# A two-layer adjacency kernel: the rows' score constants and the final tests moved to the end, one ScalarE pass per adjacency block, and records scattered later

## The chip, the cores and the metric

The kernel runs on one core of a Trainium2 chip. The metric is device time in microseconds, the median of several executions. Lower is better. TensorE is called PE in the profile, VectorE DVE, ScalarE ACT, GpSimd POOL and SyncE SP.

## The reference

There are 2708 nodes with 1024 features, a sparse 0/1 adjacency matrix, and two layers:

```python
# layer 0
q = x @ W_q.T + b_q;  k = x @ W_k.T + b_k;  v = x @ W_v.T + b_v
z = (q @ k.T) / 32 * adj
z = where(z == 0, -10000, z)
x = layernorm(x + relu(softmax(z, axis=1) @ v))
# layer 1
x = layernorm(x + adj @ (x @ weight) + bias)
```

## The kernel before

The function `sparse_part` treats the adjacency as lists of neighbours; after it a branch on `flag` runs `dense_part` only if one of the tests made by the sparse part has failed. With these inputs the branch is not taken. The nodes are 22 blocks of 128 rows (the last has 20). The stages overlap and are written in this order:

1. **Weights.** W_q and W_k are turned on TensorE, and M = scale W_q^T W_k is formed by 28 half-size products (`product_of_m`, seven for each of four blocks, the scheme of Strassen and Winograd).
2. **Listing.** `list_columns` handles a block of adjacency rows: it is loaded in six column ranges, each followed by eight ones that serve as an end mark. ScalarE counts the nonzero elements with a Sign pass, and looks for negative ones with a Relu pass (`neg`). VectorE finds up to eight ones in each range (`max_index`), and sorts their places into `keys`. Three buffers `a` go round, and `a_tile` has GpSimd set the ones in each of them anew. Sixteen blocks (`EARLY`) are listed during M's products, the rest during y's first pairs.
3. **Sorting.** Rows are ordered by degree in two families (blocks 0 to 7 and the rest): `sort_begin`, `sort_end`, then `records_out` scatters each row's record of neighbours into `tab_ds` from GpSimd, and reads it back as `tabs` and `tab0`. `records_back` makes masks of them.
4. **y = x M + a row.** Four pairs of blocks go through `y_pair`, in seven half products each, of which the third to sixth use sums of x (`y_sums_of`, on GpSimd) and four also differences of M (`t1` to `t4`, on VectorE). The other blocks go through `y_block`. The row of biases adds `y_col`. The score of row i with neighbour j is y_i . x_j plus a constant of row i, c_i = x_i . u + b, where u comes from b_k and W_q. Before, c_i is formed beside the pairs: `load_rows_of_c` loads x again, `row_constants` multiplies it by `u_bc`, and c_i is stored behind y's row, which is therefore 1028 elements wide (`YW`).
5. **Layer 0.** For each sorted block, `attend` gathers the neighbours' rows of x by indirect DMA from GpSimd, forms scores, a softmax and the weighted sum on VectorE, and pairs of blocks are projected by W_v (`project_pair`). A constant of a row doesn't change its softmax; it is needed for the tests only. Rows with one neighbour (`single`, blocks 18 and 19) need no score for their result; their score is formed by a second job of `attend_one`, for the test alone.
6. **The tests** (L1348 to L1378): scores equal to zero, degrees over the slots, a maximum that is so low that masked entries would count. A matmul with ones collects them, and `values_load` gives the flag to each engine.
7. **Layer 1.** Ten units of two blocks: `sum_rows` gathers neighbours, `work1` multiplies by the weight, `finish1` normalizes and scatters the result.

Every engine takes its instructions in the order of its own queue. A scheduler fixes these orders beforehand, by program order and its own expectation of when an instruction's inputs are there; `tc.high_priority` draws evictions from PSUM (`add`) forward, and `follow(later, earlier)` makes an instruction wait for another. `products` holds the last matmul of each block or unit, `began` the first matmul of each half product. `p_tr` is a ring of three PSUM banks, `p_mm` one bank, `p_o` four banks for products. The names and lines that the prediction uses: L213 ones, L231 and L232 ScalarE's passes, L235 `max_index`, L241 part of the listing, L308 `add`, L379 to L382 `y_sums_of`, L659 in `sort_end`, L679 the scatter of records, L712 in `records_back`, L761 a sum for M, L767 a copy of M's products, L789 and L809 `t3` and `t4`, L921 scatter, L1445 layer 1's evictions.

Of the kernel before, what the change touches and what calls it, by code (L numbers as in the profile page):

```python
# [9 lines left out]
F32 = mybir.dt.float32  # L10
BF16 = mybir.dt.bfloat16
I32 = mybir.dt.int32
U16 = mybir.dt.uint16
# [7 lines left out]
P = 128  # L21
# [59 lines left out]
def sparse_part(ctx, tc, x, xT, adj, wqT, wkT, wvT, bq, bk, bv, w1, b1, out):  # L81
# [14 lines left out]
    YW = D + 4  # L96
# [5 lines left out]
    y_ds = [dram.tile([n, YW], F32, name=f"y{f}_d") for f, n in enumerate((FAMILY * P, N - FAMILY * P))]  # L102
# [8 lines left out]
    with es:  # L111
# [81 lines left out]
        neg = lists.tile([P, NB], F32, name="neg")  # L193
        keys = lists.tile([P, NB, KEYS], F32, name="keys")
        nc.vector.memset(cnt, float(8 * RANGES))
        nc.vector.memset(neg, 0.0)
# [12 lines left out]
        def a_tile():  # L209

            a = la.tile([P, AW], F32, name="a")
            for i in range(RANGES):
                nc.gpsimd.memset(a[:, cuts[i + 1] + 8 * i:cuts[i + 1] + 8 * i + 8], 1.0)  # L213
            return a

        def load_adj():
            b = len(loaded)
            if b < NB:
                a = a_tile()
                for i in range(RANGES):  # L220
                    load_rows(a[:, cuts[i] + 8 * i:cuts[i + 1] + 8 * i], adj[:, cuts[i]:cuts[i + 1]], b * P, rows[b])
                loaded.append(a)
# [3 lines left out]
        def list_columns():  # L226
# [4 lines left out]
            nc.scalar.activation(junk[:n], a[:n], AF.Sign, accum_out=cnt[:n, b:b + 1])  # L231
            nc.scalar.activation(junk[:n], a[:n], AF.Relu, scale=-1.0, accum_out=neg[:n, b:b + 1])  # L232
# [15 lines left out]
        b_bc = a_tile()  # L248
# [224 lines left out]
        top2 = const.tile([P, 2], F32, name="top2")  # L473
        bad = const.tile([P, 1], F32, name="bad")
# [148 lines left out]
        def sort_begin(f):  # L623
# [9 lines left out]
            nc.vector.tensor_scalar(capn, neg[:, bs], 0.0, 1.0e6, op0=ALU.is_gt, op1=ALU.mult)  # L633
            nc.vector.tensor_add(deg[:, bs], deg[:, bs], capn)
# [11 lines left out]
        def sort_end(f, behind=None):  # L646
            b0, nb = families[f]
            bs, NKB = slice(b0, b0 + nb), NK * nb
            before = spare_bank()
# [75 lines left out]
        def product_of_m(acc, a, w, start, stop):  # L725
# [8 lines left out]
            if not sorted_ and done > FAMILY + 2 and worked > 7 * DC // 2 - 4:  # L734
                records_out(*sort_end(0, put), 0, FAMILY)
                sorted_.append(0)
# [75 lines left out]
        c_all = stat.tile([P, NB, YW - D], F32, name="c_all", bufs=1)  # L812
        nc.vector.memset(c_all, 0.0)
        y_bc = xa.tile([P, YW], F32, name="y_bc", bufs=1)
        bcast_rows(y_bc, y_col)
        u_bc = xa.tile([P, D], F32, name="u_bc", bufs=1)
        mm = p_mm.tile([P, HALF], F32, name="mm")
        nc.tensor.matmul(mm[:, :1], ones, bqk, start=True, stop=True)
        nc.vector.memset(y_bc[:, D:], 0.0)
        nc.vector.tensor_copy(y_bc[:, D:D + 1], mm[:, :1])  # L820


        deal = deal_hub()
        junkc = lists.tile([P, D], U8, name="junkc")
        c_ready, c_blocks = [], list(range(NB))

        def load_rows_of_c():
            a = la.tile([P, AW], F32, name="a")
            for k in range(2):
                b = c_blocks.pop(0)  # L830
                load_rows(a[:, k * D:(k + 1) * D], x, b * P, rows[b])
                c_ready.append((b, a[:, k * D:(k + 1) * D]))

        def row_constants(count):
            for _ in range(count):
                b, xg = c_ready.pop(0)
                n = rows[b]
                nc.vector.scalar_tensor_tensor(junkc[:n], xg[:n], 1.0, u_bc[:n], op0=ALU.mult, op1=ALU.mult,
                                               accum_out=c_all[:n, b, 0:1])
                if b in (FAMILY - 1, NB - 1):  # L840
                    f = int(b >= FAMILY)
                    b0, end = families[f][0], sum(families[f])
                    nc.vector.tensor_scalar(c_all[:, b0:end, 0], c_all[:, b0:end, 0], y_bc[:, D:D + 1], None, op0=ALU.add)
                    full = min(end, NB - 1)
                    nc.sync.dma_start(out=y_ds[f][:(full - b0) * P, D:].rearrange("(b p) e -> p b e", p=P), in_=c_all[:, b0:full])
                    if full < end:
                        nc.sync.dma_start(out=y_ds[f][(full - b0) * P:, D:], in_=c_all[:rows[full], full])
# [8 lines left out]
        for b in range(0, FAMILY, 2):  # L856
            while done < min(NB, EARLY + 4 * (b // 2 + 1)):
                list_columns()
                done += 1
            y_pair(b)  # L860
            if b == 0:
                bcast_rows(u_bc, u_col)
# [5 lines left out]
            row_constants(len(c_ready))  # L868
            for _ in range({2: 4, 4: 5, 6: 2}.get(b, 0)):
                load_rows_of_c()  # L870
# [5 lines left out]
        for b in range(FAMILY, FAMILY + 2):  # L876
# [4 lines left out]
            row_constants(len(c_ready))  # L881
            load_wv(range(2 * (b - FAMILY), 2 * (b - FAMILY) + 2))
        assert not c_ready and not c_blocks
# [32 lines left out]
        def gather_y(b):  # L916
            yg = wp.tile([P, YW], F32, name="yg")
# [96 lines left out]
        def score(yg, xg, s, n):  # L1014
            nc.vector.scalar_tensor_tensor(junkv[:n], yg[:n, :D], scale, xg[:n], op0=ALU.mult, op1=ALU.mult,  # L1015
                                           accum_out=s)

        def masked_scores(b, j0, s, yg, less):
# [3 lines left out]
            nc.vector.scalar_tensor_tensor(z, s, yg[:n, D:D + 1], less, op0=ALU.add, op1=ALU.add)  # L1022
# [6 lines left out]
        def attend(b, got):  # L1029
# [4 lines left out]
            for i, (j0, j1) in enumerate(cut):  # L1034
# [5 lines left out]
                z = masked_scores(b, j0, s[:n, :m], yg, less[:n, b, j0:j1])  # L1040
# [53 lines left out]
        def attend_one(b, got):  # L1094
# [7 lines left out]
            yg = gather_y(b)  # L1102
            xg = gather(x, b, 0, n)
            s = stat.tile([P, 1], F32, name="s1")
            score(yg, xg, s[:n], n)
            masked_scores(b, 0, s[:n], yg, less[:n, b, 0:1])
            yield
# [14 lines left out]
        def attend_shares(b, got):  # L1122
# [7 lines left out]
            yg = wp.tile([P, YW], F32, name="yg")  # L1130
            gather_at(y_ds[0][:, :], rec[:, OFF:OFF + 1], P, yg)
            for i, (j0, j1) in enumerate(pieces(J)):
# [5 lines left out]
                z = masked_scores(b, j0, s[:, :m], yg, far_less[:, j0:j1])  # L1138
# [98 lines left out]
        late_jobs = [7, 19, 18, 8, 8, 17, 8, 16, 11, 15, 10, 9, 14, 19, 13, 12, 18]  # L1237
# [110 lines left out]
        cap = stat.tile([P, NB], F32, name="cap", bufs=1)  # L1348
        for b in range(NB):
            nc.vector.memset(cap[:, b:b + 1], float(SLOTS[b]))  # L1350
        nc.vector.memset(cap[:HUB, 0:1], 1e9)
        nc.vector.memset(cap[HUB:2 * HUB, 0:1], float(ROW))
        if rows[-1] < P:
            nc.vector.memset(cap[:, NB - 1:NB], 1e9)
            nc.vector.memset(cap[:rows[-1], NB - 1:NB], float(SLOTS[-1]))
        over = stat.tile([P, NB], F32, name="over", bufs=1)
        nc.vector.tensor_tensor(over, degs, cap, op=ALU.is_gt)
        s0, b0 = slot0[single[0]], single[0]
        nc.vector.scalar_tensor_tensor(nms[:, b0:b0 + len(single)], scores[:, s0:s0 + len(single)], -1.0,
                                       valid[:, b0:b0 + len(single), 0], op0=ALU.mult, op1=ALU.mult)  # L1360

        nc.vector.tensor_scalar(scores, scores, 0.0, None, op0=ALU.is_equal)
        zero = stat.tile([P, 1], F32, name="zero", bufs=1)
        nc.vector.tensor_reduce(zero, scores, AX.X, ALU.max)
        nc.vector.tensor_max(bad, bad, zero)
        low = stat.tile([P, NB], F32, name="low", bufs=1)
# [433 lines left out]
```

## Time and profile before

| | us |
|---|---|
| median of 3 runs (1079.43 to 1086.11) | 1081.06 |
| the profiled execution | 1078.39 |
| its span, first to last instruction | 1076.7 |
| TensorE busy in it | 967.3 (90%) |
| VectorE | 854.9 (79%) |
| GpSimd | 529.4 (49%) |
| ScalarE | 432.2 (40%) |

The profile is of one execution; its own time is that of the span and 1.7 us around it. Durations below are from it. In its lines, "out<-in" are the program's tile names without buffer numbers, "x8" is a count, and brackets hold the idle time of the engine before the instruction and what ended it. A row of waits reads: who waited, for whom, us in total, times, longest.

### The profile page before, as it was taken

Reading aid. Unit: us, or ns where it says so; the run is one execution under the profiler, and the core shown is the slowest. Engines: PE = TensorE matmul, PEld = TensorE weight load, DVE = VectorE, ACT = ScalarE, POOL = GpSimd, SP = SyncE. Lnnn points to the kernel's source line nnn. Section 1 sums busy time; section 2 is a strip of 40 time slices with the busy share of each in tenths; the row PEclk is TensorE's granted clock in tenths of the full one; section 3 lists DMA queues with packets and bytes.
Section 4 is the critical chain, followed back from the end, with each engine's and each line's share of the span. In section 5 each row is a group of like instructions: output and inputs, shape, how many; then the busy total and the mean of one; then the engine's idle time right before and its main releaser. Section 6 shows DMA issues by size and latency. Waiting matters only on the chain.

```text
span 1076.7 us, 10650 instructions
## 1 busy us (share of the span) xinstructions
PE 967.3 (90%) x2697; PEld 454.8 (42%) x2697; DVE 854.9 (79%) x2071; ACT 432.2 (40%) x902; POOL 529.4 (49%) x552
## 2 busy tenths in 40 slices
PE   7998859899999798768999999999499899989893
PEld 6443424344444343333554444444254344435441
DVE  8999969996485897999999998844469777867532
ACT  4598866525221322231633333322323243353521
POOL 0441073123167774555565766210388777768510
PEclk9998979999999899888999999999799999999997
DMA  9558875799846767645645777334597699987731
GB/s 353 163 172 246 246 206 150 242 310 315 297 148 199 254 206 235 188 135 162 221 129 196 246 235 255 120 112 134 196 272 238 202 299 285 329 244 211 216 93 42
DMA packets 105782, 228.80 MB, mean 213 GB/s; under 512 B 22500, under 2 KB 49900, under 8 KB 105710
## 3 DMA queue, kind: packets, MB, share of 16 engines
q0 software_dynamic: 48192, 147.52, 43.4%
q1 hardware_dynamic: 57518, 80.50, 23.5%
q8 instruction: 23, 0.38, 0.1%
q14 instruction: 49, 0.40, 0.1%
HBM read 217.60 MB, written 33.68 MB: 233 GB/s over the span
## 4 chain that ended last, share of the span: by engine, by line
DVE 21%; issue 15%; PE 14%; DMA 12%; POOL 9%; ACT 1%; POOLq 0%; DVEq 0%
PE po L291 13%; DVE junkv L1015 4%; DMA g<-x_d,tabs 4%; POOL g L459 4%; DVE r L1072 3%; DMA g<-in_x_dram,tabs 2%; DVE t L308 2%; DMA yg<-y_d,tabs 2%; POOL xr L451 1%; DVE t L1220 1%; DVE r L1156 1%; DMA g<-x_d,tab 1%; DVE r L1408 1%; DVE part L1408 1%; POOL yg L451 1%
## 5 line engine op out<-in xcount | busy, mean ns | idle before, releaser
L366 PE MATMUL po<-m,xt 128*128 128x512 f32 x416 | 185.3, 606 | 10.5 <-DVE yo L308 10.4
L291 PE MATMUL po<-t,s_all 128*128 128x512 f32 x320 | 150.2, 613 | 14.8 <-DVE xr L308 10.4
L1015 DVE SCALAR_TENSOR_TENSOR junkv<-yg,g 128x1024 uint8<-128x1024 f32 x108 | 131.9, 1221 | 38.6 <-DMA g<-in_x_dram,tabs 18.7
L459 POOL DMA_INDIRECT g<-in_x_dram,tabs x84 | 108.9, 1296 | 61.2 <-issue 12.8
L366 PEld LDWEIGHTS po<-m,xt 128*128 128x128 f32 x416 | 79.9, 194 | 113.2 <-issue 97.1
L1408 DVE SCALAR_TENSOR_TENSOR r<-g,valid,r 128x1024 f32<-128x1024 f32 x77 | 98.1, 1280 | 15.4 <-DMA g<-x_d,tabs 14.1
L291 PEld LDWEIGHTS po<-t,s_all 128*128 128x128 f32 x320 | 61.6, 195 | 98.7 <-issue 72.7
L459 POOL DMA_INDIRECT g<-x_d,tabs x66 | 76.8, 1164 | 23.2 <-issue 16.5
L977 ACT ACTIVATE junks<-t,lnm 128x1024 uint8<-128x1024 f32 (+1 forms) x40 | 45.9, 1148 | 104.5 <-DVE lnm L975 103.4
L935 ACT COPY rT<-tr 128x512 f32<-128x512 f32 x76 | 41.5, 588 | 109.3 <-PE tr L934 107.9
L235 DVE FIND_INDEX8 at_a<-ones,a 128x8 uint16<-128x83 f32 (+3 forms) x132 | 82.6, 628 | 0.0
L1072 DVE SCALAR_TENSOR_TENSOR r<-g,pr,r 128x1024 f32<-128x1024 f32 x64 | 81.6, 1279 | 0.6 <-ACT r L1070 0.3
L291 PE MATMUL po<-wv,s_all 128*128 128x512 f32 x160 | 75.4, 615 | 4.1 <-DVE s_all L1195 3.7
L440 ACT ACTIVATE junka<-xt 128x128 f32<-128x128 f32 x168 | 51.6, 307 | 64.9 <-PE po L291 33.4
L291 PE MATMUL po<-w,rT 128*128 128x512 f32 x160 | 73.7, 602 | 2.0 <-DVE t L1445 2.0
L291 PE MATMUL po<-t,rT 128*128 128x512 f32 x160 | 73.9, 604 | 0.0
L291 PE MATMUL po<-w,s_all 128*128 128x512 f32 x160 | 72.2, 592 | 0.0
L291 PE MATMUL po<-wv,rT 128*128 128x512 f32 x160 | 70.6, 592 | 0.0
L231 ACT ACTIVATE junk<-a 128x2756 uint8<-128x2756 f32 (+1 forms) x22 | 55.1, 2502 | 29.2 <-DMA a<-in_adj_dram 13.7
L990 ACT ACTIVATE t<-t,nmr,rstd 128x1024 f32<-128x1024 f32 (+1 forms) x40 | 48.7, 1237 | 35.4 <-DVE nmr L989 32.9
L213 POOL MEMSET a<- 128x8 f32 x138 | 6.2, 107 | 112.8 <-DVE junk L282 39.4
L921 POOL DMA_INDIRECT x_d<-t,tabs x22 | 27.4, 1246 | 60.6 <-ACT t L990 52.6
(395 smaller groups left out, 1751.3 us busy)
## 6 DMA issues: line engine op xcount, KB each, us to landing
xt<-in_xT_dram SPq DMA_DIRECT2D x21, 512.0 KB, 6.3
y_d<-yo SPq DMA_DIRECT2D x21, 512.0 KB, 5.0
a<-in_x_dram SPq DMA_DIRECT2D x21, 512.0 KB, 5.9
a<-in_adj_dram SPq DMA_DIRECT2D x21, 413.5 KB, 5.6
a<-in_adj_dram SPq DMA_DIRECT2D x21, 338.5 KB, 4.4
a<-in_adj_dram SPq DMA_DIRECT2D x21, 263.5 KB, 4.4
wq_i<-in_wqT_dram SPq DMA_DIRECT2D x8, 512.0 KB, 6.4
wk_i<-in_wkT_dram SPq DMA_DIRECT2D x8, 512.0 KB, 10.2
```

The costliest lines, as they stand in the source:

```text
L231: nc.scalar.activation(junk[:n], a[:n], AF.Sign, accum_out=cnt[:n, b:b + 1])
L235: nc.vector.max_index(at[:n, i], ones[:n, :8], a[:n, cuts[i] + 8 * i:cuts[i + 1] + 8 * i + 8])
L291: put = nc.tensor.matmul(acc, a[:, k], w[:, k], start=start and k == 0, stop=stop and k == DC // 2 - 1, skip_group_check=True)
L366: put = nc.tensor.matmul(po, xts[b][:, c, :], m_q[c // 4][h][:, c % 4], start=(c == 0), stop=(c == DC - 1))
L440: put = nc.scalar.activation(junka[:, :xt.shape[2]], xt[:, c, :], AF.Copy, accum_out=xs[:, c, b:b + 1])
L459: nc.gpsimd.indirect_dma_start(out=dst[:n], out_offset=None, in_=src, in_offset=bass.IndirectOffsetOnAxis(ap=at, axis=0), bounds_check=N - ...
L935: nc.scalar.copy(rT[:, g * 4:g * 4 + 4, :], tr)
L977: nc.scalar.activation(junks[:n], t[:n], AF.Square, bias=nm[:n], accum_out=vs[:n])
L990: applied.append(nc.scalar.activation(t[:n], t[:n], AF.Identity, bias=nmr[:n], scale=rstd[:n]))
L1015: nc.vector.scalar_tensor_tensor(junkv[:n], yg[:n, :D], scale, xg[:n], op0=ALU.mult, op1=ALU.mult, accum_out=s)
L1072: nc.vector.scalar_tensor_tensor(r[:n], xg[j][:n], pr[:n, j:j + 1], r[:n], op0=ALU.mult, op1=ALU.add)
L1408: put = nc.vector.scalar_tensor_tensor(r[:n], xg[:n], ok[:n, j:j + 1], r[:n], op0=ALU.mult, op1=ALU.add)
```

## The change

- **One ScalarE pass per block.** The Relu pass and `neg` are gone. The Sign pass reads the same bits as unsigned integers, so that a negative number counts as well as a positive one; whether this reading holds is tested once with -1 (`minus`, `seen`).
- **Ones set once.** The three buffers `a` are fixed tiles, and the ones behind the ranges are set when a buffer is first used.
- **First records later.** `sort_end(0)` stays in M's products, but `records_out` for the first family is called after `y_pair(0)`, behind the first matmul of that pair's second half product. In `sort_end(0)` the first sum takes `p_mm`'s bank instead of one of `p_tr`.
- **Rows' constants in layer 1.** The loads of x, the products with u, `c_all` and the wider rows of y are gone from stage 4; `masked_scores` adds the mask only. In the last two units of layer 1, x's rows are gathered by sorted row and multiplied by u (`c_rows`): twelve after the ninth unit's last matmul (`products[-1]`), eleven after the tenth's. `u_bc` is formed in the eighth unit.
- **Single blocks' scores** are formed in the last two units as well (`single_scores`), not in layer 0.
- **The tests** come after the last `finish1`, and add `c_rows` to the scores, slot by slot, before they compare them.

```diff
-            nc.scalar.activation(junk[:n], a[:n], AF.Sign, accum_out=cnt[:n, b:b + 1])
-            nc.scalar.activation(junk[:n], a[:n], AF.Relu, scale=-1.0, accum_out=neg[:n, b:b + 1])
+            nc.scalar.activation(junk[:n], a[:n].bitcast(U32), AF.Sign, accum_out=cnt[:n, b:b + 1])
...
-        def a_tile():
-            a = la.tile([P, AW], F32, name="a")
+        a_bufs = [la.tile([P, AW], F32, name=f"a{k}", bufs=1) for k in range(3)]
+        def ones_behind_ranges(a):
             for i in range(RANGES):
                 nc.gpsimd.memset(a[:, cuts[i + 1] + 8 * i:cuts[i + 1] + 8 * i + 8], 1.0)
...
-                a = a_tile()
+                a = a_bufs[b % 3]
+                if b < 3:
+                    ones_behind_ranges(a)
...
-            before = spare_bank()
+            before = spare_bank() if f else p_mm.tile([P, HALF], F32, name="mm")
...
-                records_out(*sort_end(0, put), 0, FAMILY)
-                sorted_.append(0)
+                sorted_.append(sort_end(0, put))
...
+            first = len(began)
             y_pair(b)
             if b == 0:
-                bcast_rows(u_bc, u_col)
+                records_out(*sorted_[0], 0, FAMILY, began[first + 1])
                 records_back(0)
...
-            row_constants(len(c_ready))
-            for _ in range({2: 4, 4: 5, 6: 2}.get(b, 0)):
-                load_rows_of_c()
...
-            nc.vector.scalar_tensor_tensor(z, s, yg[:n, D:D + 1], less, op0=ALU.add, op1=ALU.add)
+            nc.vector.tensor_add(z, s, less)
...
-        late_jobs = [7, 19, 18, 8, 8, 17, 8, 16, 11, 15, 10, 9, 14, 19, 13, 12, 18]
+        late_jobs = [7, 19, 18, 8, 8, 17, 8, 16, 11, 15, 10, 9, 14, 13, 12]
...
+        def row_constants(ks, behind):
+            for k in ks:
+                n = P if k in (0, NB) else rows[k]
+                at = rec_h[:, ROW:ROW + 1] if k == NB else tab0[:, ROW:ROW + 1] if k == 0 else tabs[:n, k, ROW:ROW + 1]
+                xg = gather_at(x, at, n, g_tile(), behind=behind)
+                nc.vector.scalar_tensor_tensor(junkv[:n], xg[:n], 1.0, u_bc[:n], op0=ALU.mult, op1=ALU.mult,
+                                               accum_out=c_rows[:n, k:k + 1])
+
+        def single_scores(b):
+            n = rows[b]
+            yg = gather_at(y_ds[b >= FAMILY][:, :], tabs[:n, b, OFF:OFF + 1], n, g_tile())
+            xg = gather(x, b, 0, n)
+            s = stat.tile([P, 1], F32, name="s1")
+            score(yg, xg, s[:n], n)
+            masked_scores(b, 0, s[:n], less[:n, b, 0:1])
...
             pending = list(zip(unit, *work1(unit, *turned1.pop(i), xrs.pop(i))))
+            if i == len(units) - 3:
+                u_bc = wp.tile([P, D], F32, name="r", bufs=RB)
+                bcast_rows(u_bc, u_col)
+            if i >= len(units) - 2:
+                row_constants(range(i % 2, NB + 1, 2), products[-1])
+                single_scores(single[i % 2])
...
         for p in pending:
             finish1(*p)
+        cap = stat.tile([P, NB], F32, name="cap", bufs=1)
...
+        mm = p_mm.tile([P, HALF], F32, name="mm")
+        nc.tensor.matmul(mm[:, :1], ones, bqk, start=True, stop=True)
+        nc.vector.tensor_scalar(c_rows, c_rows, mm[:, :1], None, op0=ALU.add)
+        for k, (b, slots) in enumerate(list(enumerate(SLOTS)) + [("hub", HUB_SLOTS)]):
+            if slots:
+                z = scores[:, slot0[b]:slot0[b] + slots]
+                nc.vector.tensor_scalar(z, z, c_rows[:, k:k + 1], 0.0, op0=ALU.add, op1=ALU.is_equal)
+        nc.vector.tensor_sub(nms, nms, c_rows[:, :NB])
...
+        nc.vector.tensor_scalar(flag, mm[:1, 0, :1], 0.0, None, op0=ALU.is_gt)
+        raised = nc.values_load(flag, min_val=0, max_val=1, skip_runtime_bounds_check_because="a comparison's result")
```

## The prediction, made before the changed kernel ran

> **What bounds the kernel now.** I read the totals first, then the busy time by stage (cut at the steps of TensorE's work), then the waits inside the stage the change touches, then the queues of GpSimd and VectorE there, last the end of the span.
>
> ```profile
> PE 967.3 (90%) x2697; PEld 454.8 (42%) x2697; DVE 854.9 (79%) x2071; ACT 432.2 (40%) x902; POOL 529.4 (49%) x552
> ```
>
> TensorE is the bound on average; ScalarE, whose passes are halved, is at 40%. By stage (columns: stretch, length, busy time of PE, PEld, DVE, ACT, POOL, clock, DMA share, GB/s):
>
> ```profile
> 27.00:131.35 104.35, 99.02 (x235) 44.18 (x234) 104.09 (x363) 81.95 (x73) 27.71 (x100) 0.97 0.67 204
> 131.35:157.00 25.65, 9.86 (x27) 4.77 (x24) 22.06 (x82) 20.92 (x28) 15.99 (x23) 0.81 0.85 248
> 176.30:204.80 28.50, 25.69 (x64) 10.98 (x63) 28.40 (x116) 24.80 (x66) 6.31 (x11) 1.00 0.70 212
> 513.00:764.00 251.00, 243.94 (x693) 116.53 (x691) 204.58 (x485) 94.71 (x178) 114.81 (x88) 0.99 0.56 183
> 1017.00:1060.30 43.30, 43.16 (x96) 18.75 (x96) 15.69 (x49) 11.97 (x18) 7.86 (x7) 0.96 0.28 75
> ```
>
> To see: while the weights' product M is formed (27 to 131) VectorE is as full as TensorE (104.09 of 104.35); its load is the listing of adjacency columns. From 131 to 157 TensorE works 9.86 of 25.65. The last unit's time (1017 on) is TensorE alone. What TensorE waited for between 131 and 256:
>
> ```profile
> PE po L291 <- POOL y_s L380: 10.9, 1, 10.9
> PE tr L187 <- DVE upto L659: 4.9, 1, 4.9
> PE po L291 <- DVE yo L308: 3.9, 6, 1.2
> ```
>
> The first is GpSimd's queue, the order in it being the cause:
>
> ```profile
> 139.12 1.14 POOL L679 DMA_INDIRECT tab_d<-rec,pos_i  x1 [2.93 <-DVE at_a L235]
> 148.23 2.79 POOL L679 DMA_INDIRECT tab_d<-rec,pos_i  x1 [0.30 <-issue]
> 151.26 3.28 POOL L379 TENSOR_TENSOR y_s<-xt 128x512 f32<-128x512 f32 x1
> ```
>
> Eight record scatters (139.1 to 151.0) stand ahead of the sums that y's first pair needs. What would be late next, on VectorE:
>
> ```profile
> 147.89 2.28 DVE L789 TENSOR_TENSOR y_t<-y_t,m 128x2048 f32<-128x2048 f32 x1
> 151.15 2.26 DVE L809 TENSOR_TENSOR y_t<-m,y_t 128x2048 f32<-128x2048 f32 x1
> 162.63 0.69 DVE L308 TENSOR_TENSOR yo<-po,y_bc 128x512 f32<-128x512 f32 x1 [9.21 <-PE po L291]
> ```
>
> The weights' differences t3 (L789) and t4 (L809) end at 150.2 and 153.4, only behind the sixteenth listed block. The end of the span:
>
> ```profile
> 1060.33 0.69 DVE L1445 SCALAR_TENSOR_TENSOR t<-po,xr 128x512 f32<-128x512 f32 x1 [1.43 <-PE po L291]
> 1064.75 0.95 POOL L921 DMA_INDIRECT out_dram<-t,tabs  x1 [5.17 <-ACT t L1008]
> L77 POOLq INC_SWDGE_SEM  x1: 1620/1620/1620, 1068.3 to 1068.3; - x1
> L1796 POOLq DRAIN  x3: 50/107/5867, 1069.9 to 1076.4; - x3
> ```
>
> The last matmul ends at 1060.3, and 16.4 us follow: the last block's norm and scatter (landed about 1068), 1.62 and 5.87 us of GpSimd's closing.
>
> **What the Trainium skill says.** "TensorE: Matmul & The Clock Gate", What's actually happening: after an idle window of about 3.4 us the array runs at half clock until it has been busy as long. The trace agrees: after the 10.9 us wait 24 matmuls took 12.35 us, against 24 x 0.429 = 10.3. "SBUF — State Buffer", SBUF: two separate sides: a GpSimd operation and a VectorE one with two SBUF inputs lock each other out. Agrees: L241 took 1.18 us beside GpSimd's L761 at 61.1, 0.20 at 136.5. "ScalarE: Activation LUTs", The pipeline for one element: 0.833 ns an element, whatever the function. A pass over 2756 would be 2.30 us and a fixed part; the rows show 2.50. It says nothing of uint32 input. "DMA: Bandwidth & Descriptors", Where 436 GB/s comes from: 435 GB/s at the ports, some 358 at HBM. The nine gathers at 254.9 to 266 ran with 408 GB/s moving (266 to 270), so the measurement stands above the lower figure.
>
> **The change part by part.** Sums are against the profiled execution (1078.39 us, span 1076.7); the median shown is 2.67 us above it.
>
> *One ScalarE pass.* 22 x (2.50 + 0.19) = 59 us of ScalarE go. In the M stage ScalarE's copy L767 came late behind listing passes: TensorE waited 5.3 us at 95, and ran cold after it. That alone could end M 4 to 7 us sooner. The uint32 Sign pass isn't in the trace: no faster than the 2.30 above, and taken at 2.50; at 5.0 the saving is gone, with nothing lost.
>
> *Ones set once.* 114 of 138 memsets of 0.1 us leave GpSimd, and each load then waits for VectorE and ScalarE only, and by ranges. Cost nothing; VectorE never starved for blocks there, so no gain by itself.
>
> *Records later; another bank for sort_end.* The scatters (8 x 1.28 + 1.5 = 11.9 us) go behind the second product of pair 0, so the sums come first. Their input xt was issued at 129.0; xt lands in 6.3 (its issue row), so 135.3; three operations at 1.28 give S1 at about 139.5. The transposes of y_bc no longer wait for L659 (4.9). TensorE then does products 1 and 2 by 137 to 139, product 3 from 140. Product 5 needs t3. VectorE was full from 27 on, and the change takes next to nothing from it before 147, so t3 stays: 147.89 + 2.28, and two evictions of 0.68 now fall ahead of it: 151.5. Products 5 to 7 are 3 x 8 x 0.429 = 10.3: pair 0 ends at 161.8, where it ended at 176.3. **Gain 14.5**, not the 24 of all waits. If the listing of one more block (its searches, 3.77, and small operations: about 5.5 us) is ordered ahead of t3, 9 remain; if t3 is drawn ahead, 19. The tables arrive later (they landed by 166, first read at 185.9, gathers begin at 254.9): covered, or about 5 us if VectorE reaches L712 first.
>
> *Row constants out of y's pairs.* 22 products of 1.30 leave VectorE between 202 and 257, 10.6 MB of loads leave SP's queue, and y's rows are 4096 bytes. Pairs 2, 4 and 6 took 28.5, 25.5 and 25.0 where 56 matmuls of 0.429 are 24.0: 6.1 lost, of it 0.9 the transposes of u_bc. Pair 2's is the listing, which stays; I take **3** of it, 0 to 6. The 0.9 comes back in layer 1. Later stages follow TensorE and only shift.
>
> *Two single blocks' scores out of layer 0.* 3 us of VectorE and four gathers; TensorE is at 244 of 251 there: **1**, between -1 and 3.
>
> *The old tests* were 1.6 us at 691 to 692.7 on an idle VectorE, and a matmul at 761 that nothing waited for: nothing.
>
> *Twelve constants after unit 8's last matmul.* GpSimd issues 12 gathers at 1.30 in the last unit's 24 us, where it was busy 7.9 of 43: they fit. The 12 products (15.6 us) fit VectorE too, but stand in its queue ahead of evictions while a gather is in flight (5.7 from issue to landing). TensorE has four banks, two products' slack: **+1.5**, 0 to 4.
>
> *Eleven constants after unit 9's last matmul.* This is bare, as no matmul is left. Zero is the last matmul's end. Eleven gathers at 1.30: the last is issued at 13.2, lands at 18.4 (I take 5.2, between 4.45 for the first gather of layer 1 and 5.7), its product ends at 19.8. Then c_rows' addition 0.2; 21 small operations at 0.10 spacing 2.1; subtractions and the old chain of tests 2.1; matmul and flag 0.7: 24.9. Before, the flag was known at 762; now GpSimd's load of it (0.50), its waits (0.8) and closing (1.62 + 5.87 + 0.8) follow: 34.5 instead of 16.4. **+18.1**, between +15 (part of the drain covered) and +22. The last block's scatter, behind eleven gathers on GpSimd, lands by 21 and is hidden.
>
> Sum: -14.5 - 3 - 1 + 1.5 + 18.1 = +1.1, so 1079.5 profiled, **1082 us** against the median.
>
> **Rivals.** *Slower: VectorE's listing takes the waits' place.* ScalarE no longer spaces the blocks, so two blocks (11 us) come ahead of t3, which ends at 162.5; pair 0 then gains 3.5, and the sum is +12: 1093. It decides from the second block on. For it: VectorE is full from 27 to 153. Against it: L789's inputs were ready by then and blocks 17 on stood behind it.
> *Faster: all waits go and the end is short.* 5.3 + 4.9 + 10.9, 4 of cold clock, 5 of the pairs less what t3 keeps is 26; the end at +15, two scores 2: -13, so 1068. For it: each wait has its own row. Against it: t3's time, and POOL's 1.30 a gather.
>
> **How the numbers follow.** Cancelling 0.46, the listing 0.33, all waits gone 0.21. A difference under 1% is about what a measurement of this kernel can't tell from none, so these are also within, slower, faster. The bounds of the likeliest give 1070 to 1094; with the rivals' outer parts, 1068 to 1097.
>
> **What would show it.** Right: pair 0's last product ends about 15 us sooner, with a wait on L789's line; no row POOL y_s L380 in TensorE's waits; some 34 us between the last matmul and the end, with eleven gathers in a row at 1.3 on GpSimd. Wrong: the end under 28 us, or pair 0 ending before 156 or after 168.

## The result, and the profile after

The changed kernel takes 1093.57 us (median of 5 runs, 1091.26 to 1097.20), the kernel before 1081.38 (5 runs, 1079.43 to 1086.11): a ratio of 1.0106, 95% interval 1.0073 to 1.0139. It is about 1.1% slower. The forecast was 1082.0, no change; the time lies in its range, 1068 to 1097, near the time of the slower rival. The profiled execution of the changed kernel took 1091.26 us with a span of 1089.4, against 1078.39 and 1076.7. The ratios and their intervals in this document are not formed from the two medians beside them, and need not be their quotient.

The totals of the page, in the same columns as before:

```profile
PE 961.1 (88%) x2697; PEld 453.8 (42%) x2697; DVE 858.3 (79%) x2091; ACT 377.8 (35%) x859; POOL 544.8 (50%) x455
```

The totals don't explain 12 us more: TensorE has 6 us less work and ScalarE 54 less, and GpSimd, with 15 more, is busy for half the span. The time is in how stages hang together. Busy time by stage (stretch, length, PE, PEld, DVE, ACT, POOL, clock, DMA share, GB/s): M, pair 0's first part, pair 2, the last 43 us of matmuls, and all behind the last matmul.

```profile
27.00:131.40 104.40, 97.47 (x234) 43.37 (x233) 104.40 (x378) 50.11 (x49) 24.78 (x21) 0.97 0.74 218
131.40:157.00 25.60, 19.03 (x44) 8.33 (x43) 24.72 (x80) 13.08 (x30) 19.93 (x15) 0.80 0.67 198
167.60:193.80 26.20, 24.51 (x58) 10.44 (x57) 26.06 (x113) 12.19 (x41) 6.52 (x6) 1.00 0.38 105
1003.70:1047.00 43.30, 42.96 (x96) 18.18 (x95) 26.73 (x66) 10.73 (x17) 24.60 (x20) 0.97 0.69 208
1047.00:1089.40 42.40, 0.56 (x2) 0.50 (x2) 25.21 (x80) 2.44 (x4) 19.00 (x16) 0.55 0.59 212
```

To see: between 131 and 157 TensorE now works 19.03 us where it worked 9.86, so the waits there did go; VectorE is nearly full in each of the first three rows; and the last row is 42.40 us long with no matmul but the flag's, where 16.4 stood before. The two longest of TensorE's waits from 131 to 250:

```profile
PE po L292 <- issue: 5.9, 1, 5.9
PE po L292 <- DVE yo L309: 3.2, 4, 1.2
```

The 10.9 us wait for GpSimd's sums and the 4.9 for L659 are gone. A new one of 5.9 has come, for which the view names no releaser. GpSimd's queue shows the first part of the change at work: the sums come first, and eight scatters follow.

```profile
131.41 1.27 POOL L380 TENSOR_TENSOR y_s<-xt 128x512 f32<-128x512 f32 x1 [26.32 <-DVE keys L244]
139.90 1.13 POOL L679 DMA_INDIRECT tab_d<-rec,pos_i  x1 [3.41 <-DVE at_a L236]
151.13 2.94 POOL L679 DMA_INDIRECT tab_d<-rec,pos_i  x1 [0.30 <-issue]
```

What the new wait is for stands in VectorE's timeline, beside TensorE's (start, duration, engine, line, operation):

```profile
145.64 1.02 DVE L236 FIND_INDEX8 at_a<-ones,a 128x8 uint16<-128x835 f32 x1
146.58 0.67 DVE L309 TENSOR_TENSOR yo<-po,y_bc 128x512 f32<-128x512 f32 x1
147.70 2.28 DVE L788 TENSOR_TENSOR y_t<-y_t,m 128x2048 f32<-128x2048 f32 x1
```
```profile
140.33 1.13 PE L292 MATMUL po<-m,xt 128*128 128x512 f32 x2 [0.63 <-ACT m L779]
147.39 13.47 PE L292 MATMUL po<-y_t,y_s 128*128 128x512 f32 x24 [5.94 <-issue]
```

The third product adds onto the bank of the first, so it waits until the first is evicted (L309). That eviction stands behind the sixteenth listed block in VectorE's queue and ends at 147.25; TensorE goes on at 147.39. The 24 matmuls behind the wait took 13.47 us instead of 10.3. The granted clock, read in steps of a quarter to half a microsecond, stands at 0.50 from about 143.2 to 153.3, so it fell during the wait and stayed low for 5.9 us of work.

The end of the span, from the last gather's issue to the closing:

```profile
1063.13 0.92 POOL L452 DMA_INDIRECT g<-in_x_dram,tabs  x1 [0.30 <-issue]
1069.77 1.21 DVE L1386 SCALAR_TENSOR_TENSOR junkv<-g,r 20x1024 uint8<-20x1024 f32 x1
1073.16 1.21 DVE L977 SCALAR_TENSOR_TENSOR junkv<-g 128x1024 uint8<-128x1024 f32 x1
1077.67 0.15 DVE L1470 TENSOR_SCALAR flag<-tr 1x1 int32<-1x1 f32 x1 [0.74 <-PE tr L1469]
L78 POOLq COMPARE_BRANCH  x1: 58/58/58, 1078.4 to 1078.4; - x1
L78 POOLq INC_SWDGE_SEM  x1: 1350/1350/1350, 1082.5 to 1082.5; - x1
L1787 POOLq DRAIN  x3: 50/107/4764, 1083.8 to 1089.2; - x3
```

The last matmul ends at 1047.0. The last of eleven gathers is issued 16.2 us later, its product is done at 24.0, the flag is known at 30.8, and 11.6 us follow, of which 4.0 lie between GpSimd's branch (COMPARE_BRANCH) and its INC_SWDGE_SEM.

The difference of the two spans, stage by stage (us):

| stage | before | after | difference | predicted |
|---|---|---|---|---|
| to the end of y's pair 0 | 176.3 | 167.7 | -8.6 | -14.5 |
| pairs 2, 4, 6 | 79.0 | 76.3 | -2.7 | -3 |
| from there to the last matmul | 805.0 | 803.0 | -2.0 | +0.5 |
| last matmul to the end | 16.4 | 42.4 | +26.0 | +18.1 |
| span | 1076.7 | 1089.4 | +12.7 | +1.1 |

### The profile page after: what moved, and what is told of

It reads as the page before. It is cut to its first block, busy times and chain, and to the rows that moved or that the text cites. A ratio compares the mean times of both kernels' runs of the same rounds, so it can differ in the third digit from the quotient of the medians.

```text
span 1089.4 us, 10406 instructions
## 1 busy us (share of the span) xinstructions
PE 961.1 (88%) x2697; PEld 453.8 (42%) x2697; DVE 858.3 (79%) x2091; ACT 377.8 (35%) x859; POOL 544.8 (50%) x455
## 4 chain that ended last, share of the span: by engine, by line
DVE 34%; PE 28%; issue 14%; DMA 14%; POOL 7%; ACT 1%; SPq 0%; POOLq 0%; DVEq 0%; ACTq 0%
PE po L292 18%; PE po L367 8%; DVE at_a L236 6%; DMA g<-in_x_dram,tabs 5%; DVE junkv L977 5%; DMA g<-x_d,tabs 3%; POOL g L460 3%; DVE r L1034 3%; DVE t L309 2%; DMA a<-in_adj_dram 2%; DVE yo L309 1%; DVE t L1176 1%; POOL xr L452 1%; DVE r L1331 1%; PE tr L896 1%
## 5 line engine op out<-in xcount | busy, mean ns | idle before, releaser
L977 DVE SCALAR_TENSOR_TENSOR junkv<-yg,g 128x1024 uint8<-128x1024 f32 x106 | 129.5, 1221 | 37.4 <-DMA g<-in_x_dram,tabs 14.1
L292 PE MATMUL po<-t,s_all 128*128 128x512 f32 x320 | 148.0, 606 | 10.3 <-DVE xr L309 8.3
L233 ACT ACTIVATE junk<-a 128x2756 uint8<-128x2756 uint32 (+1 forms) x22 | 55.0, 2500 | 58.0 <-DMA a<-in_adj_dram 48.7
L292 PE MATMUL po<-wv,s_all 128*128 128x512 f32 x160 | 72.0, 593 | 0.6 <-DVE t L309 0.6
L896 PE MATMUL tr<-ident,r 128*128 128x128 f32 x304 | 42.2, 290 | 23.4 <-DVE r L1328 14.2
```

The costliest lines, as they stand in the source:

```text
L233: nc.scalar.activation(junk[:n], a[:n].bitcast(U32), AF.Sign, accum_out=cnt[:n, b:b + 1])
L292: put = nc.tensor.matmul(acc, a[:, k], w[:, k], start=start and k == 0, stop=stop and k == DC // 2 - 1, skip_group_check=True)
L896: nc.tensor.transpose(tr[:, k, :], r[:, c * P:(c + 1) * P], ident)
L977: nc.vector.scalar_tensor_tensor(junkv[:n], yg[:n], scale, xg[:n], op0=ALU.mult, op1=ALU.mult, accum_out=s)
```

## The experiments

The theory to test: the early parts gain in pair 0 what an eviction behind the listing lets them gain, and eleven bare gathers at the end take more than that back. Rivals: later stages give the early gain back; the end is long for the tests and the branch, not for the gathers; pair 0 waits for something other than the eviction. Eleven kernels ran. For each, the milestones from its profiled execution, as differences to the kernel before (us):

| kernel | pair 0's third product starts | pair 2 starts | y's block 8 starts | last matmul ends | last matmul to end |
|---|---|---|---|---|---|
| before, absolute | 157.0 | 177.0 | 255.3 | 1060.3 | 16.4 |
| changed | -9.6 | -9.4 | -11.3 | -13.3 | 42.4 |
| early parts alone | -8.5 | -8.4 | -5.5 | -5.1 | 16.4 |
| no constants | -9.5 | -9.4 | -11.3 | -15.1 | 18.5 |
| constants one unit sooner | -9.8 | -9.4 | -11.5 | -14.2 | 28.5 |
| the same, tests sooner | -9.2 | -9.2 | -11.1 | -10.2 | 29.1 |
| records only | -5.9 | -6.0 | -0.5 | +1.2 | 16.4 |
| one pass only | +0.7 | +0.6 | +0.7 | +3.9 | 16.6 |
| constants two units sooner | -10.0 | -10.4 | -11.7 | +12.3 | 14.9 |
| the same, 14 listed early | -10.8 | -9.2 | -5.7 | +13.5 | 14.9 |
| constants 5, 11, 7 | -9.3 | -10.2 | -11.7 | -10.3 | 21.7 |
| constants 8, 10, 5 | -10.2 | -10.2 | -12.2 | -0.4 | 19.9 |
| early parts, constants a pair later | -9.5 | -8.4 | -4.8 | -4.7 | 16.5 |

A caution on the fourth column: the kernels with shares 5, 11, 7 and 8, 10, 5 have the same order of instructions on TensorE up to layer 1's last units, and yet their profiled executions stood 10 us apart at the end of layer 0. So much can one execution differ from another in layer 0. The columns ahead of it agree within 1.2 us among kernels of the same early code, and the length of the end is free of it; for the time as a whole the medians and ratios count.

### The early parts alone

```diff
 (of the change, only:)
-    nc.scalar.activation(junk[:n], a[:n], AF.Relu, scale=-1.0, accum_out=neg[:n, b:b + 1])
+    (one Sign pass over a[:n].bitcast(U32); ones set in three buffers once)
-    records_out(*sort_end(0, put), 0, FAMILY)
+    records_out(*sorted_[0], 0, FAMILY, began[first + 1])    # behind pair 0's second product
```

> The kernel before with the early parts alone (one ScalarE pass, ones once, records behind pair 0's second product, the other bank); constants, single scores and tests stay where they were. Theory A (the gain lies in pair 0 and the loss in the bare end): pair 0 ends 8 to 9 us sooner as in the changed kernel, pairs 2 to 6 keep their constants and take 78 to 79 as before, 16.4 us after the last matmul: 1081.4 - 9 = 1072, 1070 to 1074. Theory B (later stages give the gain back: VectorE, full in pair 2, only passes the wait on): pair 2 grows by what pair 0 gains, 1077 to 1081.

Measured: 1073.48 us (20 runs) against 1081.32 (53 runs), ratio 0.9927, 0.9909 to 0.9944. Pair 0 gains 8.4, as theory A has it, and of that 2.9 go again in the pairs, which theory A did not have: TensorE's waits for evictions from 165 to 262 are 7.3 us here, 3.2 in the changed kernel. So this alone beats both kernels. Beside it the constants' leaving y's pairs is worth 5.8 us up to block 8, by which this kernel starts that block later than the changed one; the prediction took 3 for it. What it is worth without the early parts was not run.

### No constants

```diff
-                row_constants(range(i % 2, NB + 1, 2), products[-1])
```

> The changed kernel without the 23 constants' gathers and products (it leaves them out, c_rows stays zero; the single scores and the tests stay in the bare end). Theory A: the end loses the eleven gathers, 1.5 us each on GpSimd, so the flag comes 15 to 17 us sooner and everything before the last matmul stays (0 to 1 us): 1093.6 - 17 = 1076.5, 1075 to 1079. Theory B (the bare end is the tests, the branch and the closing, and the gathers ran beside them): 1087 to 1091.

Measured: 1066.49 us (4 runs) against 1081.32 (53 runs), ratio 0.9887, 0.9842 to 0.9932. The end shrank from 42.4 to 18.5. Theory B falls, and theory A's 17 was too small: the constants cost 23.9 us at the end. The last matmul's 1.8 us can't be told from the scatter between executions. Without them the flag is known before the last block's norm, so tests and single scores have cover again, and the branch too. The last stage of this kernel, columns as above:

```profile
1045.20:1063.70 18.50, 0.11 (x1) 0.03 (x1) 2.88 (x10) 1.31 (x3) 0.95 (x1) 0.56 0.15 59
```

GpSimd has 0.95 us of work behind the last matmul here, and 19.00 in the changed kernel.

### Constants one unit sooner, and the tests too

```diff
-            if i >= len(units) - 2:
+            if len(units) - 3 <= i < len(units) - 1:
                 row_constants(range(i % 2, NB + 1, 2), products[-1])
 (u_bc formed one unit sooner as well)
```

> The changed kernel with constants and single scores behind the products of units 7 and 8, so that they run beside the products of units 8 and 9; the tests stay last in the program. Theory A: none of the gathers is bare any more; after the last matmul 17 to 24 us remain, by whether VectorE has the tests before or after the last norm: 1093.6 - 18 to 25 = 1069 to 1076, taken 1072. Theory B (a constant's product stands in VectorE's queue ahead of evictions while its gather flies, so 23 of them cost TensorE what the end saves): the last matmul 8 us later or more, 1080 to 1086.

Measured: 1077.92 us (18 runs), ratio 0.9980, 0.9963 to 0.9997. TensorE lost nothing that can be told (last matmul -14.2), so theory B falls; but the end is still 28.5, longer than theory A's 17 to 24. GpSimd's queue says the greater part of why:

```profile
1024.69 2.68 POOL L452 DMA_INDIRECT xr<-x_d,tabs  x1 [0.30 <-issue]
1044.94 0.97 POOL L452 DMA_INDIRECT g<-in_x_dram,rec_h  x1 [0.30 <-issue]
```

From 998.8 to 1052 it issues almost without a break: 23 gathers, the two scores', the last unit's residuals and the scatters. The last constant's gather is issued 1 us before the last matmul ends. Two units of TensorE's work are as long as GpSimd's list, not longer. GpSimd isn't alone in being full: from 1046 to 1055 VectorE is busy 9.00 us of 9.00 and takes the products one by one to 1055.4, and from 1036 to 1046 the DMA engines move 408 GB/s without a pause. Which of the three holds the end here was not separated.

With the tests ordered ahead of the last norms:

```diff
-        for p in pending:
-            finish1(*p)
         cap = stat.tile([P, NB], F32, name="cap", bufs=1)
 ...
+        for p in pending:
+            finish1(*p)
         raised = nc.values_load(flag, ...)
```

> As the one before, with the tests ordered ahead of the last unit's norms. Theory A: after the last matmul remains what the kernel before had, 16.4 and up to 2 for the branch: 1093.6 - 25 = 1068.5, 1066 to 1071, so faster than both kernels. Theory B: as there, 1078 to 1084.

Measured: 1079.85 us (20 runs), ratio 0.9979, 0.9961 to 0.9997: a miss for theory A. The time lies in theory B's range, but its mechanism does not fit: the last matmul comes 3 us later than in the changed kernel, not 8. The end stayed at 29.1. By its timeline the last constant's product runs at 1058.3, 8 us after the last matmul, and the additions (L1444 and L1448 in this kernel) follow it at once: the tests' place in the program was not what held them, they wait for the constants.

### Records only, one pass only

```diff
-            before = spare_bank()
+            before = spare_bank() if f else p_mm.tile([P, HALF], F32, name="mm")
 (and the records behind pair 0's second product, as above; nothing else)
```

> The kernel before with one edit: the eight record scatters behind pair 0's second product, and sort_end's first matmul in the other bank. ScalarE keeps its two passes, the ones are set each time. Theory A (the place of the scatters in GpSimd's queue is the whole early gain): pair 0 ends 8 to 10 us sooner, the time is that of all early parts together, 1072 to 1075. Theory B (without the halved ScalarE pass the copy of y_bc and the listing come later, so that the sums are on time for nothing): pair 0 gains 4 at most, 1077 to 1080.

Measured: 1078.57 us (20 runs), ratio 0.9966, 0.9947 to 0.9986. Neither theory, though the time lies in B's range: the place of the scatters brings pair 0 forward by 6.0, two thirds of what all parts bring, and the pairs behind it hand 5.5 back, to 7.6 us of waits for evictions. The 0.3% left is at the edge of what can be told. The other early parts, one pass and the ones set once, take the time on to 1073.48 (the first experiment), which the prediction held to be nothing; which of the two does it was not tried.

```diff
-    nc.scalar.activation(junk[:n], a[:n], AF.Sign, accum_out=cnt[:n, b:b + 1])
-    nc.scalar.activation(junk[:n], a[:n], AF.Relu, scale=-1.0, accum_out=neg[:n, b:b + 1])
+    nc.scalar.activation(junk[:n], a[:n].bitcast(U32), AF.Sign, accum_out=cnt[:n, b:b + 1])
```

> The kernel before with one edit: a single ScalarE pass over the uint32 view of each block. Theory A (ScalarE is hidden; with one pass it waits for the blocks' loads where it had waited for nothing): the weights' product M ends at most 2 us away from where it ended, records and y's sums stay, 1079 to 1084. Theory B (the prediction's other reading: ScalarE's late copies of M cost TensorE 5 us and its clock): M ends 4 to 7 us sooner and the time follows, 1074 to 1077.

Measured: 1080.05 us (12 runs), ratio 0.9989, 0.9966 to 1.0012: theory A's time, no difference. The wait of TensorE for ScalarE's copies of M did not go with half of ScalarE's passes; by M's end it is 9.5 us here and was 5.3 in the kernel before. M itself ends 4.0 us later, which is more than theory A's 2 and the opposite of theory B. Little of that remains behind it, because pair 0's third product waits for GpSimd's sums in both kernels and starts only 0.7 us later:

```profile
PE tr L292 <- ACT m L766: 9.5, 2, 6.4
```

### Constants two units sooner, and 14 blocks listed early

```diff
-            if i >= len(units) - 2:
+            if len(units) - 4 <= i < len(units) - 2:
                 row_constants(range(i % 2, NB + 1, 2), products[-1])
 (tests behind unit 8's products; u_bc formed two units sooner)
```

> The changed kernel with constants and single scores behind the products of units 6 and 7, so that the last gather flies in unit 8's time, and the tests ordered behind unit 8's products. Theory A (23 gathers of 1.3 to 1.7 and their products fit beside two units of 24 us if nothing has to be ready at the end): last matmul at 1046 to 1048, 16.4 to 18.5 behind it: 1066 to 1069. Theory B (GpSimd's queue holds the last unit's sums behind the constants' gathers): last matmul 4 to 10 us later, 1071 to 1077.

Measured: 1085.85 us (20 runs), ratio 1.0044, 1.0024 to 1.0064. The end is short, 14.9, and TensorE stands still for 20 us in the middle of layer 1 (its timeline, then VectorE's):

```profile
1018.27 2.08 PE L292 MATMUL po<-w,rT 128*128 128x512 f32 x2 [20.24 <-DVE t L1368]
```
```profile
1016.18 1.23 DVE L977 SCALAR_TENSOR_TENSOR junkv<-g 128x1024 uint8<-128x1024 f32 x1 [1.37 <-DMA g<-in_x_dram,tabs]
1017.52 0.68 DVE L1368 SCALAR_TENSOR_TENSOR t<-po,xr 128x512 f32<-128x512 f32 x1
```

Twelve products of constants (997.0 to 1014.8) and the single score stand in VectorE's queue ahead of three evictions (L1368), most of them back to back. Theory A falls, and theory B's 4 to 10 us are exceeded by another mechanism: not the last unit's sums on GpSimd, but evictions on VectorE.

With 14 blocks listed early besides:

```diff
-EARLY = 16
+EARLY = 14
```

> As the one before, with 14 adjacency blocks listed by the end of M instead of 16 (EARLY 14), the rest in y's first pairs; in VectorE's queue 89 searches instead of 96 then stand ahead of t3 and t4, and about as many fewer ahead of pair 0's first eviction. Theory A (pair 0's third product waits for an eviction that stands behind the listing): the eviction runs 4 to 5 us sooner, pair 0 ends at 162 to 164 instead of 167.7, and the later pairs give back 1 to 3 of it. Theory B (it waits for what ScalarE or GpSimd does, y_bc's copy or the sums): pair 0 ends within 1 us of 167.7.

Measured: 1090.48 us (9 runs), ratio 1.0074, 1.0034 to 1.0113. In time a miss: pair 0 ends as before, and the pairs behind it, which now carry more of the listing, hand 3.5 us back. But it tells what TensorE waits for (VectorE, then TensorE):

```profile
140.93 2.28 DVE L788 TENSOR_TENSOR y_t<-y_t,m 128x2048 f32<-128x2048 f32 x1
145.44 0.68 DVE L309 TENSOR_TENSOR yo<-po,y_bc 128x512 f32<-128x512 f32 x1
```
```profile
146.27 13.46 PE L292 MATMUL po<-y_t,y_s 128*128 128x512 f32 x24 [6.40 <-DVE yo L309]
```

Here t3 was ready at 143.21, 6.8 us sooner than in the changed kernel (149.98), and TensorE still began only behind the eviction. The order in VectorE's queue merely turned round: t3 and t4 came ahead of the eviction. End of the eviction and start of the third product: 147.25 and 147.39 in the changed kernel, 146.12 and 146.27 here, 151.01 and 151.15 with the records alone, 148.35 and 148.49 with the early parts alone. The gap is 0.14 to 0.15 each time, whatever t3 does.

### The constants spread over three units

```diff
-            if i >= len(units) - 2:
-                row_constants(range(i % 2, NB + 1, 2), products[-1])
-                single_scores(single[i % 2])
+            shares = {6: range(5), 7: range(5, 16), 8: range(16, NB + 1)}
+            if i in shares:
+                row_constants(shares[i], products[-1])
+            if i in (6, 7):
+                single_scores(single[i % 2])
 (u_bc formed two units sooner)
```

> The changed kernel with the constants spread: 5 behind unit 6's products, 11 behind unit 7's, 7 behind unit 8's, each behind the last blocks' own gather; single scores behind units 6 and 7; the tests stay last. Theory A (GpSimd stood still for 8 to 10 us ahead of unit 7's end in the run with everything behind units 7 and 8; five gathers fit there, and no block of products as long as in the run behind 6 and 7 stands ahead of evictions): last matmul at 1046 to 1050, 15 to 19 behind it, 1066 to 1071, faster than all before. Theory B (any product of a constant in VectorE's queue ahead of unit 8's evictions costs TensorE about its flight): last matmul at 1054 or later, 1073 to 1078.

Measured: 1074.88 us (20 runs) against 1081.98 (38 runs), ratio 0.9952, 0.9931 to 0.9973. Faster than the kernel before and, by 1.7% of the medians, than the changed one, but not what theory A had. The last matmul, at 1050.0, is in A's range; the time is in B's; the end is 21.7, and TensorE waits 3.4 us for an eviction shortly before it.

> The same with 8, 10 and 5. Theory A: within 2 us of the one before, since neither the end nor the evictions wait for constants: 1066 to 1071. Theory B: three more products and gathers ahead of unit 8's evictions, 1.5 to 2 us each: 3 to 6 later than the one before.

Measured: 1078.05 us (20 runs), ratio 0.9966, 0.9945 to 0.9987; 3 us above the one before by the medians, the lower edge of theory B, though the two intervals overlap. TensorE waits once for 8.8 us in the last units (TensorE, then VectorE):

```profile
1021.41 5.98 PE L292 MATMUL po<-t,s_all 128*128 128x512 f32 x8 [8.83 <-DVE xr L309]
1020.66 0.69 DVE L309 TENSOR_TENSOR xr<-po,xr 128x512 f32<-128x512 f32 x1 [5.89 <-DMA xr<-x_d,tabs]
```

This eviction adds the residual rows `xr`, and VectorE stood idle for their gather; its last product of a constant had ended at 1011.9. GpSimd issued that gather only at 1014.3, behind eight gathers of constants, the single score's two and three scatters, the last of which had waited 2.1 us for a norm. In the kernel with 5, 11 and 7 the eviction waits for its `xr` at last too; that gather was issued at 1029.0, behind eleven constants. So theory B's mechanism, a product ahead of an eviction, is not what these two traces show: the constants stand in GpSimd's queue ahead of a gather that the eviction needs. And constants ahead of evictions do not always cost: twelve behind unit 8 in the changed kernel, and all 23 behind units 7 and 8, cost TensorE nothing that can be told.

### The early parts, with the constants one pair later

```diff
-            for _ in range({2: 4, 4: 5, 6: 2}.get(b, 0)):
+            for _ in range({4: 4, 6: 5}.get(b, 0)):    # and two behind block 8
                 load_rows_of_c()
```

> The early parts alone, as in the first experiment, with the loads of x's rows for the constants one pair later (behind pairs 4 and 6 and block 8 instead of pairs 2, 4 and 6), so that no constant's product runs on VectorE while adjacency blocks are still listed. Theory A (the early parts lost 3 us of pair 0's gain in pairs 2 to 6 because listing and constants share a full VectorE): the waits for evictions after pair 0 fall from 7.3 to 4 or less, y's pairs end 8 to 11 us sooner than in the kernel before instead of 5.5, 1068 to 1071. Theory B (the loads only push the waits into the blocks behind and into layer 0's first gathers): pairs end 8 sooner, but layer 0 begins as late as before, 1073 to 1076.

Measured: 1073.66 us (4 runs) against 1084.09 (7 runs), ratio 0.9898, 0.9857 to 0.9939; against the early parts alone (1073.48, ratio 0.9927, on another chip) no difference that can be told. Both theories fall, though the time is in B's range: the waits stay (6.7 us), and block 8 starts 4.8 sooner than before instead of 8. VectorE's timeline in pair 6 shows another cause:

```profile
239.62 1.23 DVE L839 SCALAR_TENSOR_TENSOR junkc<-a,u_bc 128x1024 uint8<-128x1024 f32 x1 [3.58 <-DMA a<-in_x_dram]
243.24 1.23 DVE L839 SCALAR_TENSOR_TENSOR junkc<-a,u_bc 128x1024 uint8<-128x1024 f32 x1 [2.38 <-DMA a<-in_x_dram]
244.39 0.69 DVE L310 TENSOR_TENSOR yo<-po,yo 128x512 f32<-128x512 f32 x1
```

VectorE is not short of time there. It stands idle on a constant whose rows have not landed, with an eviction behind it, for which TensorE waits 2.95 us. In pair 6 of the early parts alone the DMA engines are busy 0.89 of the time at 267 GB/s, in the changed kernel's 0.41 at 134. That the loads' bandwidth is what makes them late is read from this and was not tried by itself.

## Why the prediction was wrong where it was

*Direction.* "Cancelling" was the likeliest; the change is 1.1% slower. Two terms of the sum were mis-sized, both the same way, by 5.9 and 7.9 us; the others differ by -2.2 together. That the time fell on the slower rival's 1093 is luck: pair 0 gained 5 us more than that rival had it, and the end took 7.9 more.

*Records later (-14.5, measured -8.6).* Right: the sums came on time (issued at 131.4 and done by 136.5), the transposes of y_bc no longer waited, no GpSimd row is left among TensorE's waits. Wrong step: "Product 3 from 140. Product 5 needs t3." The binding wait was one product earlier and on another line. Product 3 adds onto product 1's bank, whose eviction stood in VectorE's queue behind the same sixteenth block as t3. So product 3 began at 147.4. That alone would have moved product 5 from 151.5 to 147.4 + 16 x 0.429 = 154.3, so 2.8 us; the other 3.1 is, but for 0.2, TensorE's clock. The prediction named the clock gate ("TensorE: Matmul & The Clock Gate", What's actually happening, in the Trainium skill) for the old wait and then counted the matmuls behind the new one at 0.429. The same 24 matmuls took 13.47 us behind a wait of 5.94 in the changed kernel, and 10.54 behind one of 1.52 with the early parts alone: 2.9 us for the clock. The lines of three experiments (early parts alone; early parts, constants a pair later; records only):

```profile
148.49 10.54 PE L293 MATMUL po<-y_t,y_s 128*128 128x512 f32 x24 [1.52 <-DVE yo L310]
147.57 13.46 PE L293 MATMUL po<-y_t,y_s 128*128 128x512 f32 x24 [3.21 <-issue]
151.15 12.23 PE L291 MATMUL po<-y_t,y_s 128*128 128x512 f32 x24 [2.29 <-DVE yo L308]
```

The page and the traces agree that a wait is followed by matmuls at half clock; how long they last differs (3.6 us in the kernel before, 5.9 in the changed one, where the page has about 3.4). The sign named in the prediction, "a wait on L789's line", failed; the rival "VectorE's listing takes the waits' place" had the engine right, and the place (two blocks ahead of t3) and the size (3.5 of gain left) wrong. The signs of being wrong did not come either, one of them by little: pair 0 ended at 167.7, and 168 was the bound.

*One ScalarE pass.* Costed at nothing by itself, and by itself it is nothing (ratio 0.9989). The remark that ScalarE's late copies of M could end M 4 to 7 us sooner is wrong: with one pass alone TensorE waits longer for them, and M ends 4.0 us later. Beside the later records the pass and the ones set once are not nothing: together they are worth 5.1 us by the medians (1078.57 to 1073.48). The figure of 0.833 ns an element stands in "ScalarE: Activation LUTs" of the Trainium skill under Step-by-step: what each stage is for. Every uint32 pass took 2.50 us, as the prediction took it.

*Constants out of y's pairs (-3, measured -2.7).* The sum is right and hides a link. With the early parts alone the pairs hand 2.9 of pair 0's gain back; with the constants gone they don't. So the term is worth 5.8 to one who has the early parts already, which a sum of parts can't show. Two slips in the working changed nothing: the three pairs took 6.9 us more than their matmuls, not 6.1 (79.0 less 72.1), and 120 of the 138 memsets left GpSimd, not 114.

*Twelve constants behind unit 8 (+1.5).* TensorE waits 0.3 us in the last 43 us of its matmuls (42.96 of work in 43.30). They cost next to nothing where they stand, but the gathers filled GpSimd's queue to 1045, with the first two scatters after, so the eleven behind them began 1.1 us after the last matmul.

*Eleven constants and the tests behind the last matmul (+18.1, measured +26.0).* The shape was right, every link was short:

| from the last matmul's end (us) | predicted | measured |
|---|---|---|
| last gather issued | 13.2 | 16.2 |
| its product done | 19.8 | 24.0 |
| flag known | 24.9 | 30.8 |
| end | 34.5 | 42.4 |

The gathers came every 1.5 us in the mean, not every 1.30: six after 1.25, two after 1.6 and two after 2.2. What lengthens those was not tried; the DMA engines were busy for 0.89 to 1.01 of the time from 1047 to 1073, so the transfers may hold the gathers as well as GpSimd's issuing does. The flight was 6.5 us, not 5.2. Between products and flag the single score's product (1.21) and 0.13 instead of 0.10 an operation were missing. And the closing was 11.6 instead of 9.6: GpSimd's branch to the end of the program, 4.0 us to its INC_SWDGE_SEM, had lain beside the last scatter's flight before and was not in the sum, while the last two instructions took 6.1 instead of 7.5.

*The rest to the last matmul (+0.5, measured -2.0)* is within what executions differ by up to the end of layer 0 (10 us in the caution above).

## What to carry to other kernels

When a wait goes, follow the queue of the next engine instruction by instruction from there, to the first one that the waiting engine needs: an eviction that frees a bank is as binding as an operand, and it waits for what stands ahead of it. A wait of a few microseconds in TensorE's work (here from 2.3) is to be charged with the slow matmuls that can follow it. Work put behind the last matmul costs its whole chain (issue, flight, arithmetic, flag, branch); work that must stay is better put where its engine's queue has room and neither an eviction nor a gather that an eviction needs stands behind it, and the edits that need no such place are best taken alone: here the early parts by themselves gave 0.9927.

## What the runs showed of the hardware that was not expected

- TensorE's slow matmuls did not need a wait as long as the 3.4 us of "TensorE: Matmul & The Clock Gate" in the Trainium skill (What's actually happening): behind one of 3.21 us (early parts, constants a pair later) 24 matmuls took 13.46 us, as behind one of 5.94, and behind one of 2.29 (records only) 12.23. Length alone does not decide: in the first of these kernels TensorE also stood still for 2.5 us ahead of y's first product, and the 16 matmuls behind took 7.11, full speed. The clock stands at 0.50 for about 3.4 us with the records only (151.3 to 154.7), 6.8 with the constants a pair later (146.7 to 153.5) and 10.1 in the changed kernel (143.2 to 153.3): one, two and three times some 3.4.
- A Sign pass over 2756 uint32 elements took 2.50 us, as long as over f32.
- The branch that leaves the program was 58 ns in GpSimd's record, and its INC_SWDGE_SEM came 4.0 us after it; TensorE's record has the branch at 4.16 us in the changed kernel and 3.38 in the kernel before.
